# Own PSUM banks and own gelu groups for the third image's last MLP, behind the last scan of a four-layer image network

## The chip, the cores and the metric

The kernel runs on one core of a Trainium2 chip. The metric is the device time of one execution in microseconds (us), the median of several runs; lower is better. Every duration below comes from one profiled execution or from the runs shown with it.

## The reference, cut to what matters

Four images of 64x64 tokens with 128 channels go through four layers in turn. All arithmetic is in 32-bit floats.

- Layer 0: a layernorm, a projection to 2x256 channels, a 3x3 depthwise convolution, and a selective scan in four directions over the 4096 tokens. Then its output part, which this case is about: layernorm of the scan's sum over 256 channels, times a silu gate, a projection to 128 channels, a residual, and an MLP:

```python
y = _ln(jnp.transpose(y, (0, 2, 1)), onorm_w, onorm_b).reshape(Bn, Hh, Ww, DI)
y = y * _silu(z)
x = input + y @ out_proj_w
h2 = _ln(x, ln2_w, ln2_b)
h2 = jax.nn.gelu(h2 @ fc1_w + fc1_b, approximate=False) @ fc2_w + fc2_b
return x + h2
```

- Layer 1: self-attention over all 4096 tokens. Layer 2: 1x1 and 3x3 convolutions. Layer 3: attention in a 7x7 neighbourhood, then a second MLP of the same form (layernorm, 128 to 512, gelu, 512 to 128, residual).

The images do not depend on each other.

## The kernel before

**The order of the work.** The scan is the long part, bound by GpSimd and VectorE. `network` therefore works in a pipeline over images: while the scan of image n runs (`selective_scan`), `rest(n - 1)` does the remaining layers of image n - 1 in the gaps, and inside it `scan_output(n - 1)` also does the layer 3 MLP of image n - 2. Images are counted from 0 here. Nothing is left to overlap after the last scan: `rest(3)` then runs alone, and its first stage is `scan_output(3)` together with the layer 3 MLP of image 2 (`layer3_mlp`, the "third image's last MLP"). After it come layer 1, layer 2 and the attention of layer 3 for image 3, and last its MLP alone.

**The stage.** `scan_output` splits the image into eight chunks of 512 tokens, taken from the last to the first. A chunk is a generator, `chunk(c)`, with four yields, and two chunks are under way at a time. After each step of the chunks, one step of `before` (the generator `layer3_mlp`, also eight chunks) is taken. In this text the eight chunks of the scan output are called A to H in the order in which they are taken, and those of the other image's MLP M1 to M8. By line, one chunk does

- L600, 4 matmuls of 512 columns: centre y over 256 channels into two banks (`yc`); L604 on ScalarE squares them into `sq` (the tile of y), L605 on VectorE multiplies with weight and gate into `gated`;
- L612, 8 matmuls of one column for the variance (`pv`); L174 and L175 on ScalarE make 1/sqrt of it; L621 and L625, 8 matmuls of 128 columns each (`pb`, `pg`); L628 and L630 on VectorE make x;
- `layernorm_T`: L188 and L190 (statistics, VectorE), L174, L175, L192, L194 (four), L198 (four: normalize) on ScalarE, L201 (four transposes on TensorE into one bank), L202 (weight and bias, out of that bank into `xnT`);
- `mlp`: L219, 4 matmuls of 512 columns into four banks; L226, four gelu activations out of them; L233, 4 matmuls into one bank; L236, 4 matmuls that add x; L638 writes the result to `xT`.

A chunk of `layer3_mlp` loads x (L1560), runs the same `layernorm_T` and `mlp` without L236, and then L1566 (`yT`), L1569 (four transposes back), L1570 (residual) and L1571 (store).

**Banks and gelu groups.** PSUM has eight banks. The scan's pool (`ss_ps`) holds four of them: three for `dA`, one for `py`. `scan_output` has the other four in one pool, `so_p`, whose tiles (all with the tag `ps`) rotate: a new tile takes the bank of the tile four before it in program order, and waits until that one is read. Both the chunks and `layer3_mlp` draw from this one ring. Gelu stands in another ScalarE table than the exponential and logarithm of the layernorms, so the class `Together` keeps the four gelus of an MLP chunk as one group: `open` makes the first matmul of a group (L219) wait until the group before it is done, and `run` makes every gelu wait for the group's last matmul and issues the group with a high priority, with a load of the gelu table before it (L226) and of the other table after it (`exp_table`, L96). One `Together` object serves the chunks and `layer3_mlp`, so all 16 groups are in one chain.

**Who sets the order.** A scheduler that works with a model of the engines' times fixes each engine's instruction order when the program is built. At run time each engine takes its instructions strictly in that order, so an instruction that waits holds up all that stand behind it on its engine. SBUF pools are stacks on a left or a right side; a pool on the left can only be closed when those opened after it on the left are closed. The scan's pools are on the left and are closed by `scan_over` (it is `scan_ctx.close`), which `rest` calls after `scan_output`; `xT` is on the right.

Of the kernel before, what the change touches and what calls it, by code (L numbers as in the profile page):

```python
# [32 lines left out]
PSUM = bass.MemoryType.PSUM  # L33
# [39 lines left out]
def span(c, n=LC):  # L73
    return slice(c * n, (c + 1) * n)
# [88 lines left out]
def loader(tc, pool, A, layer):  # L163
    def load(name, shape, src=None):
        t = pool.tile(shape, F32, name=f"w{layer}_{name}")
        tc.nc.sync.dma_start(t, A[f"L{layer}_conv_{name}"] if src is None else src)
        return t

    return load


def rstd_of(nc, K, out, var):

    nc.scalar.activation(out, var, AF.Ln, bias=K.eps)  # L174
    nc.scalar.activation(out, out, AF.Exp, scale=-0.5)  # L175
# [29 lines left out]
def load_mlp(load):  # L205
    P = SimpleNamespace()
    P.w1, P.b1 = load("fc1_w", [128, FF]), load("fc1_b", [128, NF])
    P.w2, P.b2 = load("fc2_w", [128, NF, C]), load("fc2_b", [128, 1])
    return P
# [47 lines left out]
def token_tiles(dram, c):  # L257

    return dram[span(c), :].rearrange("(t p) c -> p t c", p=128)
# [302 lines left out]
    settle(S.unit + BEHIND)  # L562


def scan_output(tc, K, A, D, img, xT, last):

    nc = tc.nc  # L570
    with ExitStack() as ctx:
        pool = ctx.enter_context(tc.tile_pool(name="so", bufs=2))
        wpool = ctx.enter_context(tc.tile_pool(name="so_w", bufs=1))
        psum = ctx.enter_context(tc.tile_pool(name="so_p", bufs=4, space=PSUM))
        load = loader(tc, wpool, A, 0)
        onorm_w, onorm_b = load("onorm_w", [128, ND]), load("onorm_b", [128, ND])
        out_proj = load("out_proj_w", [128, ND, C])
        out_proj_b = wpool.tile([128, ND, C], F32, name="out_proj_b")
        for d in range(ND):
            nc.vector.tensor_scalar_mul(out_proj_b[:, d, :], out_proj[:, d, :], onorm_b[:, d : d + 1])  # L580
        center = wpool.tile([128, ND, 128], F32, name="center")
        nc.vector.memset(center, -1.0 / DI)
        nc.vector.tensor_add(center[:, 0, :], center[:, 0, :], K.ident)
        ln_w, ln_b = load("ln2_w", [128, 1]), load("ln2_b", [128, 1])
        P = load_mlp(load)
        together = Together(tc, K)

        def chunk(c):
            y = pool.tile([128, ND, LC], F32, name="y")
            nc.sync.dma_start(y, D.y[img][c])  # L590
            sz = pool.tile([128, ND, LC], F32, name="sz")
            nc.sync.dma_start(sz, D.sz[img][c])
            x = pool.tile([128, 4, 128], F32, name="x")
            nc.sync.dma_start(x, token_tiles(A["x"][img], c))
            gated = pool.tile([128, ND, LC], F32, name="gated", bufs=1)
            ycs = []
            for d in range(ND):
                yc = psum.tile([128, LC], F32, name="ps")
                for e in range(ND):
                    nc.tensor.matmul(yc, center[:, abs(d - e), :], y[:, e, :], start=(e == 0), stop=(e == ND - 1))  # L600
                ycs.append(yc)
            sq = y
            for d, yc in enumerate(ycs):
                nc.scalar.activation(sq[:, d, :], yc, AF.Square)  # L604
                nc.vector.scalar_tensor_tensor(  # L605
                    gated[:, d, :], yc, onorm_w[:, d : d + 1], sz[:, d, :], ALU.mult, ALU.mult
                )
            yield
            pv = psum.tile([128, 4], F32, name="pv", tag="ps")
            for t in range(4):  # L610
                for d in range(ND):
                    nc.tensor.matmul(  # L612
                        pv[:, t : t + 1], sq[:, d, span(t, 128)], K.mean_col, start=(d == 0), stop=(d == ND - 1)
                    )
            rstd = pool.tile([128, 4], F32, name="rstd")
            rstd_of(nc, K, rstd, pv)
            pb = psum.tile([128, 4, 128], F32, name="pb", tag="ps")
            pg = psum.tile([128, 4, 128], F32, name="pg", tag="ps")
            for t in range(4):
                for d in range(ND):  # L620
                    nc.tensor.matmul(  # L621
                        pb[:, t, :], sz[:, d, span(t, 128)], out_proj_b[:, d, :], start=(d == 0), stop=(d == ND - 1)
                    )
                for d in range(ND):
                    nc.tensor.matmul(  # L625
                        pg[:, t, :], gated[:, d, span(t, 128)], out_proj[:, d, :], start=(d == 0), stop=(d == ND - 1)
                    )
            nc.vector.tensor_add(x, x, pb)  # L628
            for t in range(4):
                nc.vector.scalar_tensor_tensor(  # L630
                    x[:, t, :], pg[:, t, :], rstd[:, t : t + 1], x[:, t, :], ALU.mult, ALU.add
                )
            yield
            xnT = pool.tile([128, LC], F32, name="xnT")
            layernorm_T(tc, K, pool, psum, x, ln_w, ln_b, xnT)
            yield
            po = yield from mlp(tc, K, P, pool, psum, together, xnT, x)
            nc.scalar.activation(xT[:, span(c)], po, AF.Identity, bias=P.b2)  # L638

        before = None  # L640
        if last is not None:
            before = layer3_mlp(tc, K, A, D, *last, wpool, pool, psum, together)
        elif not K.general:
            before = chain(layer0_bound(tc, K, A, wpool, psum), layer3_bound(tc, K, A, wpool, psum))
        running, todo = [], list(range(NCH - 1, -1, -1))
        while todo or running:
            if todo and len(running) < 2:
                running.append(chunk(todo.pop(0)))
            running = [r for r in running if step(r)]
            if before is not None:  # L650
                step(before)
        while before is not None and step(before):
            pass


def step(stage):

    return next(stage, stage) is None
# [893 lines left out]
def layer3_mlp(tc, K, A, D, img, out, wpool, pool, psum, together):  # L1552

    nc = tc.nc
    load = loader(tc, wpool, A, 3)
    n_w, n_b = load("norm2_g", [128, 1]), load("norm2_b", [128, 1])
    P = load_mlp(load)
    for c in range(NCH):
        x = pool.tile([128, 4, 128], F32, name="x3", bufs=3)
        nc.sync.dma_start(x, token_tiles(D.x5[img], c))  # L1560
        xnT = pool.tile([128, LC], F32, name="xnT")
        layernorm_T(tc, K, pool, psum, x, n_w, n_b, xnT)
        yield
        po = yield from mlp(tc, K, P, pool, psum, together, xnT)
        yT = pool.tile([128, LC], F32, name="yT", bufs=1)
        nc.scalar.activation(yT, po, AF.Identity, bias=P.b2)  # L1566
        pt = psum.tile([128, 4, 128], F32, name="ps")
        for t in range(4):
            nc.tensor.transpose(pt[:, t, :], yT[:, span(t, 128)], K.ident)  # L1569
        nc.vector.tensor_add(x, x, pt)  # L1570
        nc.sync.dma_start(token_tiles(out, c), x)  # L1571
        yield
# [11 lines left out]
def transposed(ctx, tc):  # L1584
    return ctx.enter_context(tc.tile_pool(name="xT", bufs=1, side="right")).tile([128, NT], F32, name="xT")


def rest(tc, K, A, D, img, last, scan_over=None):


    wide = scan_over is not None
    with ExitStack() as ctx:
        xT = transposed(ctx, tc)
        scan_output(tc, K, A, D, img, xT, last)
        if wide:
            scan_over()
        layer1(tc, K, A, D, img, xT, wide)
        layer2(tc, K, A, D, img, xT, wide)
    layer3_attention(tc, K, A, D, img, wide)
# [153 lines left out]
```

## Time and profile before

| | |
|---|---|
| median of 3 runs | 9031.49 us (9028.09 to 9043.99) |
| the profiled execution | 9043.9 us, its span 9042.2 us |
| end of the last scan (its last `y_sum`, L556) | 7900.8 us from the span's start |
| the stage: first L600 of image 3 to first L743 of layer 1 | 7904.6 to 8199.2 us (294.6 us) |
| layer 1, layer 2, attention of layer 3, last MLP | 8199 to 8583, to 8700, to 8940, to 9042 us |

The page cuts the span into 40 slices of 226 us; each digit is the busy share in tenths. The stage is the larger part of the slice in place 36, where GpSimd (POOL) has just gone idle. Line numbers are those of the kernel before.

### The profile page before, as it was taken

Reading aid. Unit: us, or ns where it says so; the run is one execution under the profiler, and the core shown is the slowest. Engines: PE = TensorE matmul, PEld = TensorE weight load, DVE = VectorE, ACT = ScalarE, POOL = GpSimd, SP = SyncE. Lnnn points to the kernel's source line nnn. Section 1 sums busy time; section 2 is a strip of 40 time slices with the busy share of each in tenths; the row PEclk is TensorE's granted clock in tenths of the full one; section 3 lists DMA queues with packets and bytes.
Section 4 is the critical chain, followed back from the end, with each engine's and each line's share of the span. In section 5 each row is a group of like instructions: output and inputs, shape, how many; then the busy total and the mean of one; then the engine's idle time right before and its main releaser. Section 6 shows DMA issues by size and latency. Waiting matters only on the chain. (4 is left out here: it accounts for less than half of the span.)

```text
span 9042.2 us, 99354 instructions
## 1 busy us (share of the span) xinstructions
PE 7228.6 (80%) x30116; PEld 2738.4 (30%) x30116; DVE 7119.0 (79%) x8483; ACT 5646.5 (62%) x11581; POOL 7048.5 (78%) x3064
## 2 busy tenths in 40 slices
PE   5835868686788997877788988877888978888987
PEld 2211213132422232333322333333222323343333
DVE  3888878787899988988899988888899898813433
ACT  5746767675666666657766665667666666554355
POOL 5988898999899979997899979988999799800000
PEclk8757868696898998888898988888999988889989
DMA  4777676777544445565444555565445465510020
GB/s 169 254 235 238 238 243 239 252 249 267 170 166 170 163 161 198 194 213 181 156 168 167 176 181 179 200 201 165 166 160 178 146 215 186 184 51 4 7 78 29
DMA packets 716655, 1581.74 MB, mean 175 GB/s; under 512 B 203317, under 2 KB 328396, under 8 KB 711757
## 3 DMA queue, kind: packets, MB, share of 16 engines
q1 hardware_dynamic: 585805, 1399.10, 45.3%
q10 hardware_dynamic: 130304, 176.19, 5.5%
q8 instruction: 241, 3.95, 0.2%
q14 instruction: 305, 2.50, 0.1%
HBM read 1280.47 MB, written 283.59 MB: 173 GB/s over the span
## 5 line engine op out<-in xcount | busy, mean ns | idle before, releaser
L485 POOL TENSOR_TENSOR dB<-du,bc 128x1024 f32<-128x1024 f32 x2048 | 4799.3, 2372 | 699.2 <-DMA bc<-bc_dram 263.0
L491 ACT ACTIVATE dA<-dt,w_A_log 128x512 f32<-128x512 f32 x4096 | 2782.4, 691 | 606.5 <-DVE hc L493 306.1
L493 DVE TENSOR_TENSOR_SCAN dA<-dA,state,dB 128x512 f32<-128x512 f32 x2128 | 2630.1, 1272 | 291.2 <-POOL dB L485 153.9
L493 DVE TENSOR_TENSOR_SCAN hc<-dA,state,dB 128x512 f32<-128x512 f32 x1456 | 1804.6, 1267 | 299.9 <-ACT dA L491 115.3
L506 POOL TENSOR_TENSOR hc<-hc,bc 128x1024 f32<-128x1024 f32 x832 | 1969.8, 2373 | 81.0 <-ACT state L502 55.8
L498 DVE TENSOR_TENSOR hc<-dA,bc 128x512 f32<-128x512 f32 x2432 | 1566.3, 675 | 129.7 <-PE py L539 114.0
L539 PE MATMUL py<-hc,pick 128*32 128x512 f32 x8192 | 1256.6, 693 | 388.0 <-POOL hc L506 273.3
L823 PE MATMUL pa<-e,l_v 128*128 128x512 f32 x2048 | 1083.6, 662 | 24.4 <-ACT e L779 24.3
L500 ACT COPY state<-dA 128x1 f32<-128x1 f32 x2128 | 328.7, 158 | 1207.9 <-DVE hc L498 1196.5
L775 PE MATMUL pair<-l_g,l_f 32*128 32x512 f32 x2048 | 539.2, 676 | 186.7 <-ACT e L779 136.3
L779 ACT ACTIVATE e<-pair 128x1024 f32<-128x1024 f32 (+1 forms) x448 | 508.4, 1135 | 236.5 <-PE pair L775 230.4
L823 PEld LDWEIGHTS pa<-e,l_v 128*128 128x128 f32 x2048 | 380.3, 202 | 691.8 <-issue 635.0
L539 PEld LDWEIGHTS py<-hc,pick 128*32 128x32 f32 x8192 | 213.4, 117 | 1152.9 <-issue 472.7
L1281 PE MATMUL pair<-table,ident 128*128 128x512 f32 x768 | 429.5, 687 | 114.3 <-ACT e L1291 95.5
L247 PE MATMUL ps<-band,w_conv_diag 128*128 128x504 f32 (+3 forms) x1152 | 500.8, 594 | 3.5 <-ACT delta L397 3.5
L493 DVE TENSOR_TENSOR_SCAN dA<-dA,dB 128x512 f32<-128x512 f32 x304 | 357.7, 1213 | 69.8 <-POOL dB L485 50.2
L201 PE MATMUL ps<-ident,ln_xn 128*128 128x128 f32 x512 | 134.6, 359 | 305.3 <-ACT ln_xn L198 198.1
L328 POOL TENSOR_TENSOR du<-delta,xc 128x1024 f32<-128x1024 f32 x128 | 334.7, 2622 | 49.3 <-ACT delta L397 47.8
L1291 ACT ACTIVATE e<-pair 128x1024 f32<-128x1024 f32 (+1 forms) x224 | 254.4, 1136 | 167.9 <-PE pair L1285 167.5
L219 PE MATMUL ps<-xnT,w_fc_w 128*128 128x512 f32 x512 | 277.5, 675 | 72.9 <-ACT mlp_h L226 33.4
L247 PEld LDWEIGHTS ps<-band,w_conv_diag 128*128 128x128 f32 x1152 | 221.6, 193 | 282.1 <-issue 263.1
L775 PEld LDWEIGHTS pair<-l_g,l_f 32*128 32x128 f32 x2048 | 140.6, 190 | 548.3 <-ACT e L779 262.2
(274 smaller groups left out, 8583.6 us busy)
## 6 DMA issues: line engine op xcount, KB each, us to landing
bc<-bc_dram SPq DMA_DIRECT2D x1024, 512.0 KB
dt<-delta_dram SPq DMA_DIRECT2D x512, 512.0 KB
du<-du_dram SPq DMA_DIRECT2D x512, 512.0 KB
delta_dram<-delta ACTq DMA_DIRECT2D x128, 512.0 KB
du_dram<-du SPq DMA_DIRECT2D x128, 512.0 KB
table<-biasT_dram SPq DMA_DIRECT2D x72, 512.0 KB
y_first_dram<-y_sum ACTq DMA_DIRECT2D x128, 256.0 KB
y_before<-y_first_dram SPq DMA_DIRECT2D x128, 256.0 KB
```

What stands on the lines that cost most here:

```text
L247: mm = nc.tensor.matmul(out[:, r0 - row0 : r1 - row0, c0:c1], lhsT((dy + 1) * 3 + dx + 1), src[:, r0 + dy : r1 + dy, c0 + dx : c1 + dx], s ...
L328: nc.gpsimd.tensor_mul(du.rearrange("p d (a b) -> p d a b", b=H), deltas[b].rearrange("p d (a b) -> p d a b", b=H), tk,)
L485: nc.gpsimd.tensor_mul(dB, dus[pp], mid(bct[:, 0, :], 2))
L491: nc.scalar.activation(dA, dts[pp][:, g, :], AF.Exp, scale=S.A[:, k, j, pr, g : g + 1])
L493: nc.vector.tensor_tensor_scan(hg[:, order], dA[:, order], dB[:, g, order], 0.0 if i == 0 else state[:, j, pr, g : g + 1], ALU.mult, ALU.add,)
L498: mm = nc.vector.tensor_mul(hc[:, g, :], dA, bct[:, 1, :])
L506: made.append(nc.gpsimd.tensor_mul(hc, hc, mid(bct[:, 1, :], 2)))
L539: mm = nc.tensor.matmul(py[0][32 * q : 32 * q + 32, :], S.pick, hcs[q // 2][:, q % 2, :], start=(k == 1 and j == 0), stop=(j == NJS - 1),)
L775: nc.tensor.matmul(ps[:, u, :], f[quad, t // 4, span(t % 4, 128)], g[quad, c, :], start=True, stop=True)
L779: made = nc.scalar.activation(e, ps, AF.Exp)
L823: nc.tensor.matmul(pa, v[:, 8 * q + t, :], es[q], start=(t == 0 and q == 0), stop=(t == 7 and q == 3),)
L1281: nc.tensor.matmul(ps[:, u, :], K.ident, t[:, u, :], start=True, stop=False)
```

## The change

The last `scan_output` (the one that is given `scan_over`) puts its three pools on the right side. It can then close the scan's pools itself, before it makes `layer3_mlp`; it opens a second PSUM pool, `so_p2`, on the four banks that were the scan's, and a second `Together` object, and gives both to `layer3_mlp`. The chunks keep `so_p` and the first `Together` by default arguments. `rest` no longer calls `scan_over`. No operation, shape or load is added or removed.

```diff
-def scan_output(tc, K, A, D, img, xT, last):
+def scan_output(tc, K, A, D, img, xT, last, scan_over=None):
...
-        pool = ctx.enter_context(tc.tile_pool(name="so", bufs=2))
-        wpool = ctx.enter_context(tc.tile_pool(name="so_w", bufs=1))
-        psum = ctx.enter_context(tc.tile_pool(name="so_p", bufs=4, space=PSUM))
+        side = "left" if scan_over is None else "right"
+        pool = ctx.enter_context(tc.tile_pool(name="so", bufs=2, side=side))
+        wpool = ctx.enter_context(tc.tile_pool(name="so_w", bufs=1, side=side))
+        psum = ctx.enter_context(tc.tile_pool(name="so_p", bufs=4, space=PSUM, side=side))
...
-        def chunk(c):
+        def chunk(c, psum=psum, together=together):
...
         if last is not None:
+            if scan_over is not None:
+                scan_over()
+                psum = ctx.enter_context(tc.tile_pool(name="so_p2", bufs=4, space=PSUM))
+                together = Together(tc, K)
             before = layer3_mlp(tc, K, A, D, *last, wpool, pool, psum, together)
...
     with ExitStack() as ctx:
         xT = transposed(ctx, tc)
-        scan_output(tc, K, A, D, img, xT, last)
-        if wide:
-            scan_over()
+        scan_output(tc, K, A, D, img, xT, last, scan_over)
         layer1(tc, K, A, D, img, xT, wide)
```

In the built program the scheduler's order is the same as before up to the first chunk of this stage on every engine, and changes inside the stage. Behind it TensorE's order differs in a few places only: one matmul of layer 2 moved by five places, and two or three groups of layer 3's attention moved past one another. ScalarE still has 16 gelu groups with 16 table loads ahead of them and 16 after them in the stage.

## The prediction

> **What bounds the kernel now.** First the page's slices: they show where the change can act at all.
>
> ```profile
> PE   5835868686788997877788988877888978888987
> POOL 5988898999899979997899979988999799800000
> ```
>
> The scan keeps POOL at 8 or 9 tenths up to place 35; from place 36 POOL is idle and one image is left alone. The edited stage lies there, 7904.6 to 8199.2 us, so at most its 294.6 us are at stake. Next, busy times by stretch (length; then PE, weight load, DVE, ACT, POOL, each with its count; granted clock; DMA share; GB/s):
>
> ```profile
> 7904.60:8199.20 294.60, 232.76 (x864) 133.32 (x864) 48.77 (x192) 160.25 (x336) 0.00 (x0) 0.89 0.16 49
> 8199.20:8583.00 383.80, 357.85 (x1300) 143.08 (x1300) 160.88 (x107) 144.07 (x98) 0.00 (x0) 0.96 0.01 1
> ```
>
> In the stage PE is busy 79% at clock 0.89; in layer 1 behind it 93% at 0.96. ACT is busy 54%, DVE and DMA little. PE is the longest engine, but 61.8 us of it are idle. Third, the waits on PE in the stage (total us, times, longest):
>
> ```profile
> PE ps L201 <- ACT ln_xn L198: 20.1, 5, 7.6
> PE ps L201 <- ACT mlp_h L226: 12.2, 6, 3.6
> PE ps L219 <- ACT mlp_h L226: 10.8, 3, 4.1
> PE ps L1569 <- ACT yT L1566: 7.1, 8, 1.7
> PE ps L233 <- ACT mlp_h L226: 6.9, 5, 2.4
> ...
> PE pv L612 <- ACT mlp_h L226: 2.1, 1, 2.1
> ```
>
> L233 reads what gelu wrote, L1569 what L1566 wrote: data. But neither a transpose (L201), nor fc1 (L219), nor pv (L612) reads a gelu's output. They wait for a gelu because it must empty a bank, or because the chain of groups orders it: 12.2 + 10.8 + 2.1 = **25.1 us**. Last, the timeline of such a wait (start, duration, idle before):
>
> ```profile
> 7961.05 2.16 PE L219 MATMUL ps<-xnT,w_fc_w 128*128 128x512 f32 x4
> 7967.34 5.23 PE L219 MATMUL ps<-xnT,w_fc_w 128*128 128x512 f32 x8 [4.13 <-ACT mlp_h L226]
> 7973.35 3.70 PE L233 MATMUL ps<-mlp_h,w_fc_w 128*128 128x512 f32 x8 [0.78 <-ACT mlp_h L226]
> ```
>
> The second fc1 may not start before the first group's gelus end, and after the pause of 4.13 us the same 8 passes take 5.23 us instead of about 3.6. An idle PE thus costs twice.
>
> [...] 8 passes take 3.45 us normally, and 5.2 to 6.7 after pauses of 3.6 us and more. [...] here gelu starts 0.01 us after its load.
>
> **The change, part by part.**
>
> *Removed and added: no work.* The matmuls, activations and DMAs are the same, 16 gelu groups with 32 loads included. From the chain of waits, at full clock: L600 3.45 us, L612 1.7, L621 with L625 3.55, L201 0.5, L219 3.45, L233 3.45, L236 0.9: a chunk is 17.0 us of PE. One of the MLP is 0.5 + 3.45 + 3.45 + 0.5 = 7.9. Eight pairs are 8 x 24.9 = **199 us**, the floor. The stage spends 61.8 idle and 232.8 - 199 = 33.8 on a slow clock above it.
>
> *At nothing.* Giving the scan's banks to the MLP needs the scan's last reads: L498 ends at 7898.1 and L556 at 7900.8, and the MLP's first transpose came at 7913.4, so 12 us cover it; without that cover it would cost what the reads are late. The right side: the first weight load (7894.2) stands at the same place of SP's order with the same waits, as do layer 1's weights (7910). Inside the stage SP swaps a few y, sz and x loads; the latest, x for L628, is issued when L236 frees its buffer, most of a period ahead. POOL has nothing there, DVE 49 us in 295. L743 still waits for the last L1570. Later stages: under 1 us either way, as their order is almost the same.
>
> *Moved: the order inside the stage.* The built program's order has the MLP's L201 and L219 ahead of or between the chunks' work instead of behind their gelus. I walk each engine's new order with durations from the trace: on ACT L604 0.6, a layernorm's L174 to L194 1.5 (two side by side 2.5), L198 four for 1.6, L202 0.8, a gelu group 1.28 + 2.42 + 1.28, L638 and L1566 0.7; on DVE 3.1 from the end of pb and pg to statistics. The banks' ring counts too: a chunk's L201 takes the bank of its neighbour's first gelu.
>
> The second period (chunks C, D, MLP M3, M4), t from L612(C):
> - PE: L612, pb, pg of C and L1569(M2) to 5.8; L600(D) to 9.2; L201(M3) to 9.7. ACT needs L604(D) and C's statistics first, so L202(M3) ends at 11.0: **wait 1.3**. L219(M3) to 14.5.
> - L201(C), L612, pb, pg of D to 20.3, under which ACT runs gelu(M3), 14.8 to 17.2. L233(M3) to 23.8, L219(C) to 27.2, L1569(M3) to 27.7. ACT is in D's and M4's layernorms until 29.0; table; gelu(C) from 30.2, its first at 30.9. L201(D) needs that bank: **wait 3.2**. To 31.5.
> - L233(C), L236 to 35.9; L219(D), L201(M4), L219(M4) to 43.3, with gelu(D) 41.1 to 43.5 beside the last. L233(D), L600(E), L236 to 51.1, with gelu(M4) 46.1 to 48.5 beside them; L233(M4) to **54.5** = L612(E).
>
> Work 50.0, waits 4.5. From L612(C) to L612(E) it was 7986.2 to 8050.3, 64.1.
>
> The others the same way. First period, 7904.6 to L612(C): 61.8 (before 81.6), longest wait 3.5 at L201(B). Third, to L612(G): 56.7 (before 69.0), with waits of 3.2 at L201(E) and 5.3 at L201(F), which stands on PE behind L233(E) and on ACT behind two gelu groups in a row; L233(M5) and L236(E) queue behind it, and L638(E) behind those. Last, to L743: 64.9 (before 79.9), with 6.7 at L201(H), ahead of L233(G); M7 and M8 come after all chunks, so its tail (from the last L236) is some 21 us where before it was 18. Sum 61.8 + 54.5 + 56.7 + 64.9 = **237.9**.
>
> Two things the walk leaves out. Slow clock: five waits over 3 us, at the about 2.4 us that four such pauses cost before (1.8, 2.1, 3.2, 1.8, and up to 3): 12. Hand-offs, of 0.03 to 0.05 us each, and small shifts: 5, an estimate. Stage 237.9 + 12 + 5 = 255, a **gain of 40 us**. Both ends: with neither, 57; with slow clock kept in the old proportion to idle (33.8 / 61.8 x 39 = 21) and hand-offs at 10, 26.
>
> The profiled execution took 9043.9 (span 9042.2 and 1.7 around it): 9043.9 - 40 = 9004. It lies 12.4 above the median of the runs shown; I put the gain on the median: **9031.5 - 40 = 8991.5**, rounded 8991.
>
> **Rivals.** Measurement tells about 0.2%, 18 us, from no change.
> 1. *ScalarE's blocks take it back.* With two chains two gelu groups can stand side by side, 10 us in which ACT does no layernorm; PE meets it in order. For: the order has three such places, and the third period loses 5.3 there. Against: the old order has them too (7964.9 and 7972.6), and ACT's 160 us leave room in 255. If each group cost another 2 us of PE, the gain is 40 - 32 = 8: 9023.
> 2. *Slower.* L201(H)'s kind of wait, a transpose that stands on PE ahead of another chunk's L233 and waits for a layernorm queued behind a group on ACT: 6.7 idle plus 2.4 slow clock = 9.1. Five of the 16 groups in excess of the walk cancel the gain; with eight it is 40 - 73 = -33: 9064. Against: the orders show two, and both are in the sum.
> 3. *PE closes up altogether.* If [...]the waits halve: 199 + 20 = 219, gain 75: 8956. Against: the waits of the walk are data and order, not banks.
> 4. *It does not do what it says*, the MLP still in the old ring: 9031. The order excludes nearly all of this, as L219 of both stand next to each other without a gelu between them.
>
> **How the numbers follow.** Forecast (gain 18 to 65) 0.77; rival 3 (more) 0.08; rivals 1 and 4 (within 18) 0.11; slower 0.04. Range 8966 to 9014 holds the forecast with its two ends and the upper part of rival 1; it leaves out rivals 2 to 4. Faster 0.85, same 0.11, slower 0.04.
>
> **What would show it.** First L600 to first L743 near 255 us; PE busy there down from 232.8 to about 215, idle from 62 to about 40, clock above 0.89; L201, L219 and L612 waiting for mlp_h nearly gone from PE's list, but for L201(B) and L201(D), and ln_xn before L201 left as the largest wait; 32 table loads; layer 1 on unchanged. Wrong if the stage is over 277 us or L201 waits for ln_xn over 35 us in all; or if another stage moved by more than 5 us.

## The result and the profile after

The kernel takes **8984.04 us** (median of 5, 8976.0 to 8993.72) against 9028.09 us (median of 5 runs of the kernel before, 9026.76 to 9043.99): ratio **0.9945, interval 0.9934 to 0.9955**, or 44 to 50 us less. The forecast was 8991 and a gain of 40.

The profiled execution took 8980.37 us, span 8978.6. In the new file the lines of this stage stand a little lower: L600 became L602, L604 L606, L612 L614, L621 L623, L625 L627, L638 L640, L743 L749, L1566 L1572, L1569 L1575; L198 to L236 kept their numbers. The page's slices of the kernel after:

```profile
PE   5835868686788997888788888777888988888987
POOL 5988898999899979998799979988899889910000
```

A slice is now 224.5 us instead of 226, so the scan's end falls into place 36 (POOL's 1) and the digits of the last five slices can't be laid on those of before one for one. The stage has to be cut out by its own marks. Busy times of the kernel after by stretch (length; PE, weight load, DVE, ACT, POOL, each with its count; granted clock; DMA share; GB/s), first the whole stage, then its pieces up to L614(C), L614(E), L614(G), the end of the last L236 and L749, then everything behind:

```profile
7892.40:8136.00 243.60, 212.92 (x866) 125.41 (x866) 48.34 (x192) 159.64 (x336) 0.00 (x0) 0.95 0.19 59
7892.40:7952.80 60.40, 55.87 (x223) 31.91 (x223) 13.98 (x57) 43.10 (x96) 0.00 (x0) 0.97 0.33 104
7952.80:8007.00 54.20, 50.36 (x218) 30.04 (x217) 11.07 (x40) 36.76 (x73) 0.00 (x0) 1.00 0.22 68
8007.00:8067.20 60.20, 51.98 (x210) 32.40 (x209) 11.89 (x48) 36.41 (x79) 0.00 (x0) 0.91 0.19 62
8067.20:8113.60 46.40, 38.47 (x178) 24.33 (x177) 10.03 (x45) 30.00 (x71) 0.00 (x0) 0.89 0.02 6
8113.60:8136.00 22.40, 16.24 (x46) 6.73 (x44) 1.38 (x2) 13.36 (x18) 0.00 (x0) 1.00 0.04 12
8136.00:8978.60 842.60, 731.61 (x3508) 317.43 (x3508) 304.08 (x357) 397.88 (x504) 0.00 (x0) 0.91 0.09 31
```

The stage went from 294.6 to **243.6 us, 51.0 less**. ACT does the same 160 us as before. PE's idle time fell from 61.8 to 30.7, and its busy time from 232.8 to 212.9, though its work is the same. So 31.1 of the 51.0 us are waits. Most of the other 19.9 are clock, 0.89 to 0.95: by the clock records in the two traces PE was busy at half clock for 53.5 us before and for 20.1 after, and half of that is counted as lost, 26.7 and 10.1, a difference of 16.6 (eight passes of L233 took 6.35 us, 5.5 of them at clock 0.50, where they take 3.60 at 1.00). The last 3.3 are not traced to one cause; some of it is how busy time is counted, as eight passes read 3.70 us behind a pause and 3.60 elsewhere, and there are 17 pauses instead of 30.

The two profiled executions differ by 9043.9 - 8980.4 = 63.5 us. 51.0 is the stage, 0.4 lies behind it (843.0 to 842.6), and about 12 lies ahead of it: the scan ended at 7888.7 instead of 7900.8, with the same instruction order on every engine up to there. Over all the profiles of this study the scan ended between 7874.3 and 7902.2 us, so those 12 us are spread from run to run, not gain. The ratio times the median gives 49.7.

The waits on PE in the stage, kernel after (total us, times, longest):

```profile
PE ps L201 <- ACT ln_xn L198: 9.2, 2, 6.5
PE ps L233 <- ACT mlp_h L226: 7.8, 5, 4.2
PE ps L219 <- ACT xnT L202: 5.6, 5, 1.7
PE ps L201 <- ACT mlp_h L226: 5.5, 2, 2.8
PE ps L602 <- DMA y<-y_dram: 4.4, 1, 4.4
PE ps L1575 <- ACT yT L1572: 1.6, 2, 0.8
```

Of the 25.1 us in which a transpose, fc1 or pv waited for a gelu whose result it doesn't read, 5.5 are left: two waits of L201. L219 and L614 no longer wait for a gelu at all. The other large item, L201 behind a layernorm (ln_xn), also fell, 20.1 to 9.2, and the return transposes (L1569, now L1575) from 7.1 to 1.6. So 19.6 of the 31.1 us less idle are waits for a bank or a group; the rest are other waits, which fell as the order of the instructions changed (see 4). What is left is nearly all data: gelu to fc2, layernorm to transpose, `xnT` to fc1. (The 4.4 of L602 lie ahead of the stage's first matmul.)

### The profile page after: what moved, and what is told of

The parts are those of the page before. It is cut to its first block, busy times and chain, and to the rows that moved or that the text cites. A ratio compares the mean times of both kernels' runs of the same rounds, so it can differ in the third digit from the quotient of the medians.

```text
span 8978.6 us, 99358 instructions
## 1 busy us (share of the span) xinstructions
PE 7201.0 (80%) x30116; PEld 2731.9 (30%) x30116; DVE 7114.0 (79%) x8483; ACT 5647.9 (63%) x11581; POOL 7046.0 (78%) x3064
## 5 line engine op out<-in xcount | busy, mean ns | idle before, releaser
L201 PE MATMUL ps<-ident,ln_xn 128*128 128x128 f32 x512 | 135.5, 360 | 289.4 <-ACT ln_xn L198 213.3
L219 PE MATMUL ps<-xnT,w_fc_w 128*128 128x512 f32 x512 | 276.2, 674 | 69.3 <-ACT mlp_h L226 24.4
```

The lines of the kernel that those rows point to most:

```text
L219: mm = nc.tensor.matmul(ph, P.w1[:, f * 128 : (f + 1) * 128], xnT, start=True, stop=True)
```

## The experiments

The theory: the time lay in four banks shared by two streams that don't depend on each other, with the shared chain of gelu groups a small second part. The rivals: that it lay mainly in the chain; that it lay in the order which the scheduler happens to find, with any other order as good; that the new pools' places in SBUF do it; that ScalarE's gelu blocks, not the banks, set most of the waits. "Stage" is from the first centring matmul to layer 1's first matmul in one profiled execution.

| kernel | median us (runs) | before, same chip (runs) | ratio (interval) | stage us |
|---|---|---|---|---|
| the changed kernel | 8984.04 (5) | 9028.09 (5) | 0.9945 (0.9934 to 0.9955) | 243.6 |
| 1 banks alone | 8982.67 (6) | 9036.71 (27) | 0.9941 (0.9927 to 0.9956) | 247.4 |
| 2 chain alone | 9021.69 (22) | 9036.71 (27) | 0.9983 (0.9977 to 0.999) | 288.5 |
| 3 sides alone | 9026.85 (13) | 9028.03 (17) | 0.9995 (0.9987 to 1.0004) | 295.0 |
| 4 one ring of eight | 8999.42 (6) | 9036.71 (27) | 0.996 (0.9945 to 0.9974) | 265.9 |
| 5 relu, before | 9006.64 (1) | 9028.03 (17) | - | 272.7 |
| 6 relu, after | 8976.68 (1) | 9028.03 (17) | - | 235.3 |
| 7 MLP 4 steps ahead | 8970.67 (6) | 9036.71 (27) | 0.9928 (0.9913 to 0.9942) | 239.9 |
| 8 MLP 6 steps ahead | 8968.39 (5) | 9028.03 (17) | 0.9941 (0.9927 to 0.9955) | 241.4 |
| 9 later second chunk | 8991.12 (5) | 9033.53 (25) | 0.9956 (0.9943 to 0.997) | 251.3 |
| 10 the same, 4 ahead | 8973.14 (5) | 9033.53 (25) | 0.9933 (0.9919 to 0.9947) | 241.8 |
| 11 later chunk, before | 9028.35 (21) | 9033.53 (25) | 0.9994 (0.9987 to 1.0001) | 291.7 |

**1. The banks alone.** The changed kernel without the second chain: the MLP has its four banks, and all 16 gelu groups stay in one chain.

```diff
                 psum = ctx.enter_context(tc.tile_pool(name="so_p2", bufs=4, space=PSUM))
-                together = Together(tc, K)
```

> The MLP of the third image gets the scan's four banks, but stays in the one chain of gelu groups. Theory 1 (the banks are the cause: what PE waited for were banks that gelus had to empty): the stage from the first centring matmul to layer 1 takes 240 to 255 us as in the changed kernel, and the time is 40 to 55 us under the kernel before. Theory 2 (the chain of groups is the cause: fc1 of one MLP may not start before the gelus of the other end): stage 275 to 295 us, at most 20 us under the kernel before, and fc1 (L219) waits 8 us or more for mlp_h as before. Theory 3 (each gives a part): 15 to 40 us under.

The stage takes 247.4 us, 47.2 less than before and 3.8 more than the full change. The waits on PE in the stage of this kernel:

```profile
PE ps L233 <- ACT mlp_h L226: 8.8, 5, 3.5
PE ps L201 <- ACT ln_xn L198: 6.9, 2, 6.5
PE ps L201 <- ACT mlp_h L226: 5.5, 2, 2.8
...
PE ps L219 <- ACT mlp_h L226: 4.1, 1, 4.1
```

Set beside the list of the kernel after, one line is new: a single wait of L219 of 4.1 us, a group's first matmul held until the group before it is done. Other waits are shorter here, so PE is idle for only 1.8 us more than in the changed kernel (32.5) and busy for 2.1 more; together these are the 3.8. So the edit of the banks carries 47 of the 51 us of this stage, and the second chain, once the banks are there, the remaining 4. That is read from one profile each; the totals (0.9941 and 0.9945) don't tell the two kernels apart.

**2. The chain alone.** The MLP has its own `Together`, but stays in the chunks' ring of four.

```diff
-                psum = ctx.enter_context(tc.tile_pool(name="so_p2", bufs=4, space=PSUM))
                 together = Together(tc, K)
```

> The MLP of the third image has its own chain of gelu groups, but draws from the chunks' four banks; the pools lie on the right side as in the changed kernel. The order of instructions on PE differs from the kernel before at two places only. Theory 1 (banks): within 10 us of the kernel before, stage 288 to 300 us, and the 25 us of waits of L201, L219 and pv for mlp_h stay, since the ring of four banks asks for the same gelus. Theory 2 (chain): at least 25 us under the kernel before, stage under 270 us. It is the control for the sides of the pools too: a change of over 10 us without a change in the waits would speak for addresses.

The stage takes 288.5 us, 6.1 less. The waits on PE in the stage of this kernel:

```profile
PE ps L201 <- ACT ln_xn L198: 27.5, 6, 7.6
PE ps L201 <- ACT mlp_h L226: 8.6, 5, 2.1
...
PE ps L219 <- ACT mlp_h L226: 5.6, 3, 2.4
...
PE pv L614 <- ACT mlp_h L226: 0.8, 1, 0.8
```

The expectation had these waits unchanged; those for gelus fell from 25.1 to 15.0 instead. At the same time ln_xn before L201 rose from 20.1 to 27.5. The lifted order let L219 go sooner, and the next instruction that still had no bank or no layernorm took most of it back.

**3. The pools' sides alone.** The pools are on the right and the scan's are closed early, but the MLP keeps the chunks' banks and chain. The order on every engine is that of the kernel before.

```diff
                 scan_over()
-                psum = ctx.enter_context(tc.tile_pool(name="so_p2", bufs=4, space=PSUM))
-                together = Together(tc, K)
```

> The control: the pools of the last scan output stand on the right side and the scan's pools are closed early, but the MLP keeps the chunks' banks and their chain. The instruction order of every engine is that of the kernel before; only addresses differ. Theory 1 (addresses and the early close cost and bring nothing): stage 292 to 298 us, time within 8 us of the kernel before. Rival (part of the gain of the changed kernel and of the kernel with an own chain alone is a matter of addresses): 10 to 20 us under the kernel before, with the stage or a later stage shorter at unchanged waits.

The stage takes 295.0 us (294.6 before), and the waits are the old ones to within 1.5 us:

```profile
PE ps L201 <- ACT ln_xn L198: 20.7, 5, 7.7
PE ps L219 <- ACT mlp_h L226: 10.8, 3, 4.2
PE ps L201 <- ACT mlp_h L226: 10.7, 6, 2.1
...
PE pv L614 <- ACT mlp_h L226: 2.1, 1, 2.1
```

Other addresses cost and bring nothing. This run also shows how well a stage repeats under the same order: within 0.4 us. The stages behind it do not: they took 834.3 us here at clock 0.94 and 843.0 in the kernel before at 0.92.

**4. One ring of eight banks.** The scan's pools are closed first, and both streams draw from one ring of all eight banks, with two chains.

```diff
+        if scan_over is not None:
+            scan_over()
-        psum = ctx.enter_context(tc.tile_pool(name="so_p", bufs=4, space=PSUM, side=side))
+        psum = ctx.enter_context(tc.tile_pool(name="so_p", bufs=4 if scan_over is None else 8, space=PSUM))
...
-                psum = ctx.enter_context(tc.tile_pool(name="so_p2", bufs=4, space=PSUM))
```

> After the scan's pools are closed, one PSUM pool of eight banks serves the chunks and the MLP in one ring; the chains of gelu groups are two, as in the changed kernel. Theory A (the number of banks counts: a tile waits for the one eight places before it, which is long read): stage 238 to 252 us, within 8 us of the changed kernel. Theory B (the separation counts: in a common ring a slow tile of one stream, four fc1 outputs that wait for a late gelu, still holds up the other stream): stage 258 to 285 us, 15 to 40 us slower than the changed kernel, with L201 and L219 waiting for mlp_h 10 us or more in all.

The stage takes 265.9 us, 28.7 less than before: little more than half of the gain. (By the medians, 37 against 44 us, the two kernels lie nearer, and the intervals of their ratios overlap.) The waits on PE in the stage of this kernel:

```profile
PE ps L201 <- ACT ln_xn L198: 33.6, 6, 8.2
PE ps L1575 <- ACT yT L1572: 7.1, 8, 1.7
...
PE ps L233 <- ACT mlp_h L226: 2.5, 2, 2.1
```

No transpose, fc1 or pv waits for a gelu here: with respect to the banks this is the best of all the kernels. Yet L201 waits 33.6 us for layernorms, more than before the change (20.1), six times and up to 8.2 us. The time is in the range of theory B, the mechanism is not B's. The traces show what it is: nearly the old order. 795 of the stage's 864 matmuls follow one another as in the kernel before (672 in the changed kernel), VectorE's order is the same, and the six transposes that wait stand on PE exactly where they stood. So this run comes close to the kernel before with its banks freed and its chain split: the waits for banks go, some of that time comes back as longer waits for layernorms, and 28.7 us are won. As no bank wait was left here, the other 22.3 us of the changed kernel come with the order that the scheduler built around two separate rings. The 47 us of 1 include that order; no run has it without the banks.

**5 and 6. Without the gelus' table loads.** The gelu of this stage is left out in both kernels, with a relu in its place, so that no table is loaded: 16 blocks of 1.28 + 2.42 + 1.28 us become four activations each. The edit, with the last stage's `together` made with `table=False`:

```diff
-        exp_table(self.tc, self.K, self.done)
+        if self.table:
+            exp_table(self.tc, self.K, self.done)
...
-            lambda f=f: nc.scalar.activation(hT[:, f, :], phs[f], AF.Gelu, bias=P.b1[:, f : f + 1])
+            lambda f=f: nc.scalar.activation(hT[:, f, :], phs[f], AF.Gelu if together.table else AF.Relu, bias=P.b1[:, f : f + 1])
```

In the kernel before (the edit moves its lines by one, so L201 is L202 here, L219 L220, L612 L613):

> Leaves out the gelu in this stage: relu in its place, which needs no other ScalarE table, so the 32 table loads (41 us of ScalarE) are gone; banks and chain of groups as in the kernel before. Theory 1 (PE waits for banks that are held as long as a group lasts, table loads included): the waits of L201, L219 and L612 for mlp_h fall from 25 us to 8 to 16, stage 255 to 275 us. Rival (the ring of four is short in itself, whatever the group lasts): they stay at 20 us or more, stage 278 to 294.

The stage takes 272.7 us, and ACT is busy 117.9 us instead of 160.3, in 304 instructions instead of 336. The waits on PE:

```profile
PE ps L202 <- ACT ln_xn L199: 14.4, 5, 4.8
PE ps L220 <- ACT mlp_h L227: 7.9, 3, 2.7
...
PE ps L202 <- ACT mlp_h L227: 4.7, 6, 0.8
...
PE pv L613 <- ACT mlp_h L227: 0.8, 1, 0.8
```

PE's order is the same as in the kernel before. With blocks less than half as long these waits stay, as often as before (3, 6 and 1 times), but shrink from 25.1 to 13.4 us. They are a matter of the ring and the chain, whose price is set by how long an activation group keeps them.

In the changed kernel:

> Leaves out the gelu in this stage: relu in its place, without table loads; own banks and own chain for the MLP as in the changed kernel. Theory 1 (what is left of PE's waits in the changed kernel comes from ScalarE's blocks of gelu groups): idle of PE falls from 30.7 to 10 to 18 us, the single waits of 4.2 and 6.5 us are gone, stage 220 to 232 us, and the gain of the banks is smaller than with gelu, 30 to 45 us. Rival (the rest is order and data): idle stays at 25 us or more, stage 236 to 244.

The stage takes 235.3 us. The waits on PE:

```profile
PE ps L202 <- ACT ln_xn L199: 7.9, 2, 5.1
...
PE ps L234 <- ACT mlp_h L227: 3.9, 5, 1.6
...
PE ps L202 <- ACT mlp_h L227: 2.5, 2, 1.4
```

It is 8.3 us below the changed kernel with gelu, less than was expected; PE's idle time falls from 30.7 to 22.3 us, between what the theory and the rival had named. The wait of 4.2 us is gone, but the longest, the same transpose behind a layernorm, went from 6.5 only to 5.1 us: most of it stays without the table loads. The change brings 272.7 - 235.3 = 37.4 us with relu and 51.0 with gelu. So nearly three quarters of the gain do not need long gelu blocks, as far as one run of each relu kernel tells.

**7 and 8. The MLP some steps ahead.** With its own banks, `layer3_mlp` can start before the first chunk. In the changed kernel it takes four steps first (six in the second run).

```diff
+        for _ in range(4 if scan_over is not None else 0):
+            step(before)
         while todo or running:
```

> As the changed kernel, but the MLP takes four steps before the first chunk, so that its eight chunks end about when the scan output's do. Theory A (the tail is worth its idle time: in the changed kernel PE is idle for 6.2 of the last 22.4 us, where M7 and M8 stand alone, and there are 24 us of other waits that their work can fill): stage 228 to 237 us, 7 to 16 us under the changed kernel. Theory B (the streams run against each other's in-order queues, so what is won at the tail comes back as waits at its start, where the MLP's steps stand ahead of chunk A): stage 240 to 250 us, within 5 us of the changed kernel.

> As the changed kernel, but the MLP takes six steps (two of its chunks) before the first chunk. With four steps the stage, from the end of the scan, was no shorter than in the changed kernel (247.7 against 247.3 us): what the tail won came back at the start, where the first centring waited 8.5 us behind the MLP's steps. Theory B (streams in in-order queues): the same again or worse, 247 to 258 us from the end of the scan. Theory A (a longer lead fills the tail): 236 to 244 us.

The stages are 239.9 and 241.4 us, shorter by 3.7 and 2.2. But the start was only moved, as a line of the waits on PE in the kernel with four steps shows:

```profile
PE ps L602 <- ACT ln_rstd L174: 8.5, 1, 8.5
```

The first centring matmul now stands behind a layernorm of the MLP for 8.5 us, where in the changed kernel it waited 4.4 us for its y. From the scan's end to layer 1 it is 247.7 and 249.2 us; in the changed kernel it is 247.3. Nothing is gained in this part, as theory B had it. The median with four steps, 8970.67, is nevertheless lower than the changed kernel's. In its profile the difference lies behind the stage, 828.4 us against 842.6. All profiles of the study lie between 828 and 844 us there, and 3 above, whose order is that of the kernel before, has 834.3; layer 3 also has a slightly different order here. The intervals of the ratios overlap (0.9913 to 0.9942 and 0.9934 to 0.9955), but the two other kernels with a lead (8 and 10) also lie lower, 60 us each under their kernel before where the changed kernel lies 44. Their profiles don't agree on where such a gain would arise (behind the stage they took 828.4, 836.6 and 844.3 us), so it stays open whether anything of it is the edit's.

**9, 10 and 11. Another order on purpose.** The second chunk starts two steps behind the first instead of one, which spreads their layernorms.

```diff
+        tick, started = 0, -2
         while todo or running:
-            if todo and len(running) < 2:
+            tick += 1
+            if todo and len(running) < 2 and (scan_over is None or tick - started >= 2):
                 running.append(chunk(todo.pop(0)))
+                started = tick
```

In the changed kernel:

> As the changed kernel, but a chunk is started two steps behind the other instead of one, so that in program order its layernorm transposes (L201) come behind the other chunk's L233 and L236 and no longer ahead of them. Theory 1 (what is left of PE's waits in the changed kernel is order: L201(H) stands on PE ahead of L233(G) and waits for a layernorm behind a group on ScalarE): L201 waits under 5 us for ln_xn, no wait of 6 us is left, idle of PE under 22 us, stage 222 to 236 us. Rival (it is data and ScalarE's time; another order only puts the wait elsewhere, for instance at L612, whose bank is now the one that the other chunk's gelu empties): stage 240 to 255 us.

The long waits are gone, none reaches 3 us, and idle falls from 30.7 to 28.4 us. Still the stage is longer, 251.3. The waits on PE:

```profile
PE ps L201 <- ACT ln_xn L198: 7.9, 7, 2.8
PE ps L233 <- ACT mlp_h L226: 7.0, 5, 2.1
```

PE is busy 222.9 us instead of 212.9. The timeline of PE in this kernel (start, duration, idle before) shows where:

```profile
7945.83 1.18 PE L201 MATMUL ps<-ident,ln_xn 128*128 128x128 f32 x4
7948.69 5.40 PE L233 MATMUL ps<-mlp_h,w_fc_w 128*128 128x512 f32 x8 [1.67 <-ACT mlp_h L226]
...
8005.47 0.33 PE L201 MATMUL ps<-ident,ln_xn 128*128 128x128 f32 x1 [2.79 <-ACT ln_xn L198]
8006.04 1.10 PE L201 MATMUL ps<-ident,ln_xn 128*128 128x128 f32 x3 [0.24 <-ACT ln_xn L198]
8008.01 5.35 PE L219 MATMUL ps<-xnT,w_fc_w 128*128 128x512 f32 x8 [0.87 <-ACT xnT L202]
...
8094.17 0.66 PE L1578 MATMUL ps<-ident,yT 128*128 128x128 f32 x4 [0.89 <-ACT yT L1575]
8096.03 0.33 PE L201 MATMUL ps<-ident,ln_xn 128*128 128x128 f32 x1 [1.21 <-ACT ln_xn L198]
8096.20 5.30 PE L602 MATMUL ps<-y,center 128*128 128x512 f32 x8
```

Three times eight passes (four matmuls of 512 columns) take 5.3 to 5.4 us instead of 3.60 (in two of them the granted clock was 0.50, from 7950 to 7952 us and from 8098 to 8100), and ahead of them lies no long pause, but short ones with only a few transposes between: 1.67 us, or 2.79, 0.24 and 0.87, or 0.89 and 1.21. PE is busy 10 us more, and idle only 2.3 us less. By the clock record 29.6 us of its busy time are at half clock (20.1 in the changed kernel), which costs 4.7 of the 10. The rest is time that counts as busy at full clock; some of it are transposes that come one by one, as their layernorm ends (the first line: four in 1.18 us, elsewhere 0.60). Together they more than take back what the shorter pauses give. Theory 1 fails; the stage lies in the rival's range, but the wait that the rival named, L614 for a gelu, is only 1.8 us.

The same together with four steps ahead:

> The same start two steps apart, and the MLP four steps ahead. Theory 1: with the regular order the MLP's lead fills the tail without waits between; from the end of the scan 232 to 242 us, a little under the two-step start alone or equal to it. Rival: as the lead before (247.7 against 247.3 us without it), no gain over the two-step start alone, or 3 to 8 us slower by the wait of the first centring.

8973.14 us, but with runs from 8960.25 to 8993.61; 249.4 us from the scan's end to layer 1, 2 more than in the changed kernel and 4 less than with the later chunk alone (253.6). So the theory's range is missed, the rival's "no gain over the two-step start alone" doesn't hold either, and against the changed kernel this part gains nothing.

The same order in the kernel before, with its common ring and chain:

> The kernel before, with its four common banks and one chain, and only the start two steps apart. Theory 1 (the banks are what the order needs: with one ring of four for 18 tiles of a chunk and an MLP chunk, another order meets the same gelus): stage 285 to 310 us, at most 10 us under the kernel before. Rival (the gain of the changed kernel was a luckier order that the scheduler found, and could be had without banks): stage under 270 us.

The stage takes 291.7 us, 2.9 less than before. The waits on PE:

```profile
PE ps L201 <- ACT ln_xn L198: 30.0, 10, 6.5
PE ps L219 <- ACT mlp_h L226: 10.8, 3, 4.1
```

L219 waits for the groups exactly as long as in the kernel before. This other order without the banks doesn't bring the gain; the changed kernel's own order was not tried without them.

## Why the prediction was right, point by point

**Where it acts.** That only this stage can gain was right, by 51.0 of 51.4 us from its start to the program's end. The cover for an early close of the scan's pools held: 3 shows the closing itself at no cost.

**The mechanism.** The 25.1 us of waits for gelus were the right lines to read, but they are not the whole gain: 19.6 us of them went, and 10.9 us less waiting of L201 for layernorms and 5.5 less of the return transposes came on top, while other waits grew by 5. 1 shows the banks, with the order built around them, to carry 47 us; 4 that eight banks and two chains with nearly the old order carry 29; 2 and 11 that the chain alone and one other order alone bring 6 and 3. So banks and order act together. The prediction had read the new order from the built program and walked it, so that the order was a good one was no luck. It treated banks and chain as one; on top of the banks the chain brings 4.

**The walk.** Period by period, in us:

| | before | walked | measured |
|---|---|---|---|
| to L614(C) | 81.6 | 61.8 | 60.4 |
| to L614(E) | 64.1 | 54.5 | 54.2 |
| to L614(G) | 69.0 | 56.7 | 60.2 |
| to L749 | 79.9 | 64.9 | 68.8 |
| sum | 294.6 | 237.9 | 243.6 |

The first two came out 1.4 and 0.3 under the walk, the last two 3.5 and 3.9 above it; the tail from the last L236 took 22.4 us (forecast 21). The timeline of PE after shows the pauses that the walk had named for these two periods:

```profile
8018.97 0.33 PE L201 MATMUL ps<-ident,ln_xn 128*128 128x128 f32 x1 [2.77 <-ACT ln_xn L198]
8019.14 3.17 PE L614 MATMUL pv<-mean_col,y 128*128 128x1 f32 x16
...
8039.80 5.40 PE L233 MATMUL ps<-mlp_h,w_fc_w 128*128 128x512 f32 x8 [4.24 <-ACT mlp_h L226]
...
8095.52 0.47 PE L201 MATMUL ps<-ident,ln_xn 128*128 128x128 f32 x1 [6.47 <-ACT ln_xn L198]
```

L201(E) waits 2.77 us (walk 3.2). The pause behind two gelu groups in a row is there too, 4.24 us at L233 (walk: 5.3, at L201(F) just behind it). L201(H) waits 6.47 (walk 6.7). All three are followed by slow work: the 16 passes of L614 in 3.17 us, for which the same kernel takes 1.84 elsewhere, and 8 passes of L233 in 5.40 and, behind the last, 6.35.

**The term that was mis-sized.** The sum was PE 199 + slow clock 12 + waits 38.9 + hand-offs 5 = 255. Measured: 212.9 - 199 = 13.9 of busy time above the 199, which the prediction calls slow clock, and waits with hand-offs together 30.7 instead of 43.9. So what was off is "hand-offs 5", for which there was no room (the waits on PE's list alone make up nearly all of the 30.7), and waits that the walk took 8 us too long: the five pauses over 3 us, 21.9 in the walk, came to 19.0, and the many small ones to 11.7 instead of 17.0. That is 13.2 too much, and 1.9 too little for slow clock: 255 - 11.3 = 243.6. The forecast of 40 us thus fell short by 11 in the profile; by the medians and by the ratio, 44.1 and 49.7, by 4 to 10.

**Slow clock.** The number, 12 for 13.9, came out for the wrong reason in part. By the clock records only 10.1 of the 13.9 are clock (and 26.7 of the 33.8 before); the rest is busy time above the floor at full clock. "An idle PE costs twice" priced every pause over 3 us at 2.4. Two of the five pauses, L201(B) and L201(D), were 2.77 us and cost nothing: their periods ran at clock 0.97 and 1.00. Here is L201(D), with fc2 at full speed behind it:

```profile
7983.02 0.66 PE L201 MATMUL ps<-ident,ln_xn 128*128 128x128 f32 x4 [2.77 <-ACT mlp_h L226]
7983.60 3.70 PE L233 MATMUL ps<-mlp_h,w_fc_w 128*128 128x512 f32 x8
```

L201(E) was just as short and did cost: the clock was 0.50 from 8019.4 to 8026.2 us. And 2.0 us were lost at the start of the stage, at clock 0.50 up to 7896.5, which had no price. In the kernel before, too, half clock had set in behind pauses of only 1.82, 2.18 and 2.12 us (0.50 in the 3.3 us from 7932.9, 8001.2 and 8052.4); the prediction's reading, slow passes behind pauses of 3.6 us and more, left these out.

So the length of a pause did not decide alone. Around L201(B) and L201(D) the clock stayed at 1.00 (7925.3 to 7940.0 and 7979.6 to 8007.0 us), behind L201(E), with the same 2.77 us, it did not; and behind the short pauses of 9, of 0.89 and 1.21 us for one, it was 0.50 too. What told these cases apart was not shown. The 2.4 us per pause were the author's estimate from four pauses of the kernel before.

**What was named as a sign.** PE busy 215 (212.9), clock above 0.89 (0.95), idle 40 (30.7), L201 behind ln_xn the largest wait left (9.2), 32 table loads as before:

```profile
L226 ACT ACT_TABLE_LOAD x16 | 20.5, 1283 | 4.1 <-PE ps L219 3.8
L96 ACT ACT_TABLE_LOAD x16 | 20.5, 1283 | 0.3
```

(Groups of the stage, kernel after: instructions, busy us and mean ns, idle before.) "Later stages under 1 us" held between these two profiles, 0.4, but by chance: 3 shows them to differ by 8.7 under one order. As a test of the forecast, "another stage moved by more than 5 us" was too sharp.

**The rivals.** "ScalarE's blocks take it back" did not occur in the changed kernel, but 4 is close to it in effect: 29 us of gain instead of 51, because waits of nearly the old order for ScalarE's layernorms grew where the waits for banks went. The slower rival needed five excess waits of L201(H)'s kind; there was one, and it was in the sum. Closing up to 219 us was excluded by the waits on data, as said: 30.7 us of idle remain. That the change doesn't do what it says was refuted by the lists of waits.

## What to carry to other kernels

When two independent streams share a rotating ring of buffers, look in the list of waits for instructions that wait for a result which they don't read: those waits are the ring's or an ordering chain's, and a second ring, from banks that have become free, takes them away. Here 47 us came from four banks together with the order that the scheduler built around them, and 4 from splitting the chain. Walk the in-order queues of the built program with measured durations before judging such a change; it gave the four periods within 4 us, where the idle share of the engine alone would not have. And look at the order that comes out: the same banks as one ring of eight had no bank waits left, but nearly the old order, and little more than half of the gain in this stage.

## What the runs showed of the hardware that was not expected

- TensorE ran eight passes in 5.30 us instead of 3.60 behind pauses of 0.89 and 1.21 us with a few transposes between (9; clock 0.50 from 8098 to 8100 us), while two single pauses of 2.77 us in the changed kernel cost nothing (clock 1.00). A third of 2.77 us was followed by 6.8 us at clock 0.50.
- The same instruction order behind the stage took 834.3 us in one profile and 843.0 in another (PE busy 719.0 and 726.8, clock 0.94 and 0.92), and the scan's end moved by 28 us over the profiles, while the stage itself repeated within 0.4 us. A change in one stage is better measured in that stage than in the total.
